# A three-layer graph network on one core: root products and last node blocks at other steps, lots in another spacing, and two matrices of each lot made on ScalarE

## The chip, the cores and the metric

The kernel runs on one core of a Trainium2 chip. The metric is the device time of one execution, in microseconds. The kernel before took 2903.43 us (median of three runs, 2900.62 to 2906.98). Engines are named as in the profile: PE is TensorE (PEld its weight loads), DVE VectorE, ACT ScalarE, POOL GpSimd, SP SyncE. On POOL this kernel does almost nothing but issue indirect DMAs, 128 rows each.

## What is computed

The graph has 6,250 nodes with 256 features and 100,000 edges, sorted by their destination. Each edge has a source, a destination, 32 attributes and one of three types. Three layers follow each other, and a layer norm ends it:

```python
ew = edge_attr @ edge_w + edge_b                      # 100000 x 256, the same in all layers
for l in range(3):
    residual = x
    msg = relu(x[src] * ew)
    out = 0
    for i in range(3):                                # the edge types
        h = segment_sum(msg * (edge_type == i), dst, n)
        out = out + (h * inv_cnt[i]) @ weights[l, i]
    x = residual + relu(out + x @ roots[l] + biases[l])
return layernorm(x_in + x)
```

The destinations are drawn as 6250 u², so that early nodes have many edges and late nodes few: a block of 128 nodes at the front takes dozens of edge pairs, one at the end takes three or four.

## The kernel before

**Pairs, quads and steps.** A tile is 128 edges, a pair two tiles, a quad two pairs. A layer is a loop over steps `it`; `reduce` at step `it` treats the pair `order[it]`. Everything that the pair needs is done a fixed number of steps earlier, in the same loop:

- `gather` (nine steps ahead): two indirect DMAs on POOL (line 1378) bring the source rows of `x` into the tile `xs`; eight quads of buffers (`ROWS`) are there.
- `seed_ew` (six ahead): ACT fills a PSUM tile `ew_p`, in layer 0 with the bias (L789), later with the kept `ew` that SP loaded from DRAM (L786).
- `make_ew` (five ahead, layer 0 only): PE adds the attribute product (L815); `keep_ew` (four ahead): ACT copies it out (L771, L765), and SP stores it.
- `weigh` (three ahead): DVE multiplies `xs` by `ew_p` (L838), ACT takes the relu (L839).
- `one_hot` (two ahead): DVE compares an iota with the destination and type of each edge, one 128x120 instruction for each tile (L852).
- `reduce`: PE multiplies messages and one-hot into the PSUM tile `h_p`, either with the one-hot as weights ("turned" spans, L870, then `take` on ACT, L886, and `turn` on PE, L890) or with the messages as weights (L878). A span is a run of pairs that share one place in `h_p`; `add` on DVE (L918) adds it to `acc`.

**The zone and the lots.** The 26 quads of the first 52 pairs hit very few nodes. In layer 0 their `ew` rows are scattered by POOL into a table in DRAM (L733), sorted by the source node's block and the type. Layers 1 and 2 read them back as 39 "lots" of up to four tiles: all edges of a tile have their source in one block of `x_all`, which is in SBUF. A lot so needs no gather. For a lot, PE spreads the source numbers over partitions (`seed_ew`, L781), `choose` on DVE compares them with the partition number (L794, tile `hot`, one 128x512 instruction), `expand` on PE picks the rows of `x_all` (L801), `weigh` and `one_hot` follow as for other quads (the one-hot reads a column of the tile `zone`). A lot takes two steps of the loop (some one), in which POOL has nothing to issue.

**Node blocks.** When all edges of a block of 128 nodes are added (`starts[c]` is the step), `node_mul` on PE (L947) multiplies the block's sums by the weights in two parts, at steps s and s+2; `node_end` on DVE (L978, L981) scales and adds them at s+2 and s+4, updates `x_all`, and SP writes the block to `x_mid` in DRAM (L984), the rows that the next layer gathers. Blocks are at least four steps apart. Block 48 is the short last one (106 rows), block 1 is finished after all others. The first six pairs of the next layer (twelve gathers, `gather_early`) wait for all blocks but 1, and a product on PE adds block 1's rows to them (`complete`, L830, L832); the gathers after these twelve wait for block 1's write too. In layer 2 there is a norm in place of the write (L987 to L1001).

**Root products.** `x @ roots` of a block is a transpose on PE (`root_turn`, L923) at its step, a copy on ACT two steps on (L927), a product on PE three on (`root_mul`, L931), and an addition on DVE six on (`root_keep`, L934). One PSUM buffer serves them all. Products are six steps apart at least; 22 results are held.

**What sets the order.** No scheduler moves instructions: each engine issues them as the loop writes them. The steps come from functions at the end of the file: `places_of` (between which pairs the zone's quads and the lots go), `spans_of`, `stages` (when a span is taken, turned and added), `schedule` (the order and `starts`). Layer 0 has 391 steps, layers 1 and 2 have 414 each.

## Time and profile before

| | |
|---|---|
| median of three runs | 2903.43 us |
| the profiled execution | 2903.96 us, span 2902.2 us, granted clock 0.948 |
| layer 0, by the gathers on POOL | from the start to 1142 us |
| layer 1 | 1159 to 2008 us |
| layer 2 | 2018 to 2883 us, then the last 19 us without a gather |
| indirect DMAs on POOL | 1332 + 770 + 24 + 12 gathers and 104 scatters, 2242 in all |

A row of a group reads: line, engine, operation, tile written <- tiles read, shape, count | busy time in us, mean ns of one | idle time of the engine before them, and what ended most of it. A row of the timeline reads: start, duration, engine, line, operation, tiles, and in brackets the idle time before it and what ended that. In a table of windows each row is a stretch of time, with the busy us and the number of instructions (x) of each engine.

### The profile page before, as it was taken

Reading aid. Unit: us, or ns where it says so; the run is one execution under the profiler, and the core shown is the slowest. Engines: PE = TensorE matmul, PEld = TensorE weight load, DVE = VectorE, ACT = ScalarE, POOL = GpSimd, SP = SyncE. Lnnn points to the kernel's source line nnn. Section 1 sums busy time; section 2 is a strip of 40 time slices with the busy share of each in tenths; the row PEclk is TensorE's granted clock in tenths of the full one; section 3 lists DMA queues with packets and bytes.
Section 4 is the critical chain, followed back from the end, with each engine's and each line's share of the span. In section 5 each row is a group of like instructions: output and inputs, shape, how many; then the busy total and the mean of one; then the engine's idle time right before and its main releaser. Section 6 shows DMA issues by size and latency. Waiting matters only on the chain. (4 is left out here: it accounts for less than half of the span.)

```text
span 2902.2 us, 44132 instructions
## 1 busy us (share of the span) xinstructions
PE 2409.1 (83%) x13302; PEld 1880.6 (65%) x13302; DVE 2207.5 (76%) x5612; ACT 1708.1 (59%) x2220; POOL 2138.6 (74%) x2253
## 2 busy tenths in 40 slices
PE   5799988888988789788898888777888888878776
PEld 2466656555666566577777777665666767767665
DVE  7777766766656576677878888776788888888986
ACT  5677766666666667455655555444555555555654
POOL 7676777777777775777777777776777777767775
PEclk9899998999889999999999999898999999999998
DMA  7898665556555666887777777676777777777765
GB/s 237 280 328 272 207 198 190 189 185 196 185 192 187 196 211 202 267 262 240 256 242 243 246 237 257 215 223 195 269 255 262 255 256 240 244 227 233 249 227 156
DMA packets 285411, 668.25 MB, mean 230 GB/s; under 512 B 50555, under 2 KB 142509, under 8 KB 285165
## 3 DMA queue, kind: packets, MB, share of 16 engines
q1 hardware_dynamic: 170112, 362.98, 35.9%
q0 software_dynamic: 107616, 294.11, 33.9%
q10 hardware_dynamic: 7436, 8.24, 0.9%
q8 instruction: 110, 1.80, 0.3%
q14 instruction: 137, 1.11, 0.1%
HBM read 528.50 MB, written 136.63 MB: 229 GB/s over the span
## 5 line engine op out<-in xcount | busy, mean ns | idle before, releaser
L1378 POOL DMA_INDIRECT xs<-x_mid,src_r x1332 | 1265.3, 950 | 420.1 <-issue 343.1
L1378 POOL DMA_INDIRECT xs<-in_x_dram,src_io x770 | 734.9, 954 | 243.1 <-issue 211.8
L839 ACT ACTIVATE xs<-xs 128x1024 f32<-128x1024 f32 x533 | 559.5, 1050 | 582.8 <-DVE xs L838 561.0
L838 DVE TENSOR_TENSOR xs<-ew_p,xs 128x1024 f32<-128x1024 f32 x533 | 646.5, 1213 | 314.3 <-ACT keep L771 176.3
L878 PE MATMUL h_p<-oh,xs 128*128 128x120 f32 x4768 | 692.5, 293 | 202.7 <-DVE acc L918 105.4
L878 PEld LDWEIGHTS h_p<-oh,xs 128*128 128x128 f32 x4768 | 641.3, 203 | 304.9 <-DVE acc L918 112.4
L852 DVE TENSOR_SCALAR oh<-iota_w,seg_o 128x120 f32<-128x120 f32 x2138 | 568.2, 328 | 0.0
L870 PE MATMUL h_p<-xs,oh 128*120 128x256 f32 x1868 | 517.7, 405 | 41.5 <-issue 14.7
L947 PE MATMUL o_p<-w_sb,acc 128*128 128x256 f32 (+1 forms) x1752 | 456.1, 397 | 64.8 <-DVE x_root L978 56.6
L918 DVE TENSOR_TENSOR acc<-h_p,acc 128x240 f32 (+1 forms) x764 | 338.9, 445 | 113.5 <-PE o_p L947 45.7
L947 PEld LDWEIGHTS o_p<-w_sb,acc 128*128 128x128 f32 (+1 forms) x1752 | 323.6, 195 | 141.5 <-DVE x_root L978 73.9
L870 PEld LDWEIGHTS h_p<-xs,oh 128*120 128x120 f32 x1868 | 319.5, 189 | 146.6 <-issue 30.0
L786 ACT ACTIVATE ew_p<-ew_s 128x1024 f32<-128x1024 f32 (+1 forms) x340 | 343.3, 1010 | 12.7 <-DMA ew_s<-ew_all 12.7
L771 ACT ACTIVATE keep<-ew_p 128x1024 f32<-128x1024 f32 x170 | 173.2, 1019 | 226.1 <-issue 115.5
L978 DVE SCALAR_TENSOR_TENSOR x_root<-o_p,inv,x_root 128x256 f32<-128x256 f32 (+1 forms) x438 | 210.5, 480 | 43.0 <-PE o_p L947 36.1
L839 ACT ACTIVATE zone<-zone 128x1024 f32<-128x1024 f32 (+1 forms) x78 | 78.8, 1010 | 223.9 <-DVE zone L838 223.9
L815 PE MATMUL ew_p<-ew_sb,at 64*128 64x512 f32 x630 | 199.0, 710 | 11.8 <-ACT ew_p L789 11.7
L789 ACT ACTIVATE ew_p<-seed 128x1024 f32<-128x1024 f32 (+1 forms) x194 | 198.5, 1023 | 0.0
L931 PE MATMUL r_p<-r_sb,t_s 128*128 128x256 f32 x588 | 158.7, 392 | 21.7 <-ACT t_s L927 21.4
L838 DVE TENSOR_TENSOR zone<-ew_p,zone 128x1024 f32<-128x1024 f32 (+1 forms) x78 | 90.6, 1162 | 107.5 <-PE ew_p L801 107.3
L870 PE MATMUL h_p<-zone,oh 128*120 128x256 f32 x576 | 148.0, 387 | 11.6 <-DVE acc L918 7.0
L801 PE MATMUL ew_p<-x_all,hot 128*128 128x256 f32 x588 | 150.6, 401 | 7.6 <-DVE hot L794 7.4
(178 smaller groups left out, 2340.8 us busy)
## 6 DMA issues: line engine op xcount, KB each, us to landing
ew_s<-ew_all SPq DMA_DIRECT2D x338, 512.0 KB
ew_all<-keep SPq DMA_DIRECT2D x169, 512.0 KB
zone<-zone_table SPq DMA_DIRECT2D x72, 516.0 KB
xs<-x_mid,src_r POOLq DMA_INDIRECT x1332
zone_table<-blank SPq DMA_DIRECT2D x21, 677.2 KB
xs<-in_x_dram,src_io POOLq DMA_INDIRECT x770
x_mid<-x_all SPq DMA_DIRECT2D x96, 128.0 KB
at<-in_attr_laid_dram SPq DMA_DIRECT2D x40, 256.0 KB
```

The costliest lines, as they stand in the source:

```text
L786: nc.scalar.activation(ew_ps[q][:, :n], ew_ss[q][:, :n], AF.Copy)
L789: nc.scalar.activation(ew_ps[q][:, :n], seed[:, None, None, :].to_broadcast([P, n, 2, D]), AF.Copy)
L815: nc.tensor.matmul(ew_ps[q][:, k].rearrange("p i d -> p (i d)"), at[half, :], ew_sb[half].rearrange("p i d -> p (i d)"), start=False, stop ...
L838: nc.vector.tensor_mul(there, ew_ps[q][:, pairs.start:pairs.stop, :n], there)
L839: nc.scalar.activation(there, there, AF.Relu)
L852: nc.vector.tensor_scalar(ohs[q][:, i, :], iota_w[:, :, :WIN], at, None, op0=ALU.is_equal)
L870: nc.tensor.matmul(h_p[:WK, :D], ohs[u // 2][:, t, :], rows_of(u, i), start=(i == 0 and first), stop=(i == n - 1 and closes(u)), skip_grou ...
L878: nc.tensor.matmul(h_p[:, d * WK:(d + 1) * WK], rows_of(u, i)[:, d * P:(d + 1) * P] if d < DC else full_ones, (ohs if d < DC else oh_bs)[u ...
L918: nc.vector.tensor_tensor(there, h_ps[span][:, :CH * WK].rearrange("p (c r w) -> p c r w", c=CH, r=R), there, op=ALU.add)
L947: nc.tensor.matmul(o_p[:n, j, :], acc[:, d, r, slot:slot + n], w_sb[:, r * DC + d, :], start=(d == 0), stop=(d == DC - 1))
L978: nc.vector.scalar_tensor_tensor(root, o_p[:n, j, :], inv[:n, c, r:r + 1], root, op0=ALU.mult, op1=ALU.add)
L1378: nc.gpsimd.indirect_dma_start(out=xs[:, u % 2, i, :], out_offset=None, in_=x_rows[:, :], in_offset=bass.IndirectOffsetOnAxis(ap=src_i[:, ...
```

## The change

**Root products of layer 0.** They stood at steps 5, 11, 17 and on, six apart, the last at 293. Now they stand at 20, 27, 34 and on, seven apart, the last at 356. In layers 1 and 2 the rule is the old one.

**Last blocks.** The blocks 44 to 48 are done at a quicker pace: `paces` gives 1 for them and 2 for the others; the second part follows after one step instead of two, the end after two instead of four, and the blocks are three steps apart. In layer 0 block 48 starts at step 378 (382 before) and ends at 380 (386 before). In layers 1 and 2 it starts at 402 (405) and ends at 404 (409), while block 0 moves from step 319 to 352. A new border at pair 60 cuts the last span, which ran over seven pairs (58 to 65): now (58, 60) stands alone and (60, 66) is a turned span. In layers 1 and 2 both are added one step after the point where the one was, and block 1 starts at 416 instead of 415. The span of the pairs' upper end (390, 391) is added at once.

**Lots.** Up to the 20th the places are nearly the old ones. From there the distance grows faster: before, the 30th lot stood before pair 254 and the 39th before pair 310; now they stand before 260 and 342. Before pair 288 or at it there were 36 lots, now 34.

**Matrices of a lot.** `choose` and, for lots, `one_hot` leave DVE. ACT computes relu(1 - |a - b|), which is 1 where two whole numbers are equal and 0 elsewhere: for `choose` one Abs and one Relu over 128x512, for the one-hot an Abs of 128x120 for each tile and one Relu over all (128x480).

```diff
@@ choose
-            nc.vector.tensor_scalar(hot[q][:, :n].rearrange("p i e -> p (i e)"),
-                                    ew_ps[q][:, 0].rearrange("p i d -> p (i d)")[:, :n * P],
-                                    node_i[:, 0:1], None, op0=ALU.is_equal)
+            there = hot[q][:, :n].rearrange("p i e -> p (i e)")
+            nc.scalar.activation(there, ew_ps[q][:, 0].rearrange("p i d -> p (i d)")[:, :n * P], AF.Abs, bias=node_i[:, 0:1], scale=-1.0)
+            nc.scalar.activation(there, there, AF.Relu, bias=one_f, scale=-1.0)
@@ one_hot
+            if q in zone:
+                for i in range(n):
+                    nc.scalar.activation(ohs[q][:, i, :].rearrange("p (r w) -> p r w", r=R), iota_w[:, :, :WIN], AF.Abs,
+                                         bias=zone[q][:, i // 2, i % 2, D:D + 1], scale=-1.0)
+                nc.scalar.activation(ohs[q][:, :n], ohs[q][:, :n], AF.Relu, bias=one_f, scale=-1.0)
+                return
@@ layer
+        next_at = {s + paces(c, NT): c for s, c in node_at.items()}
+        over_at = {s + 2 * paces(c, NT): c for s, c in node_at.items()}
...
-            step = max(3 + int((steps - 110) * (1 - (1 - j / NT) ** 0.5)), max(root_at, default=-1) + 6)
+            step = ROOT_AT + ROOT_EVERY * j if l == 0 else 3 + int((steps - 110) * (1 - (1 - j / NT) ** 0.5))
+            step = max(step, max(root_at, default=-1) + 6)
...
-            if it - 2 in node_at:
-                node_end(node_at[it - 2], 0)
-            if it - 4 in node_at:
-                node_end(node_at[it - 4], 1)
...
+            if it in next_at:
+                node_end(next_at[it], 0)
+            if it in over_at:
+                node_end(over_at[it], 1)
...
-LOT_SPACE = 4.5
-LOT_MORE = 0.04
+LOT_RATE = 0.215
+LOT_SLOWER = 0.000264
+ROOT_AT = 20
+ROOT_EVERY = 7
+QUICK = 5
@@ spans_of
-    stops = {K, last, middle, *quads, *lots}
+    stops = {K, last, last + 2, middle, *quads, *lots}
@@ stages
+        if spans[group[-1]][1] == -(-E // 256):
+            by = 0
@@
+def paces(c, NT):
+    return 1 if c >= NT - QUICK else 2
@@ schedule
-        step = starts[c] = max(done[c] + 2, step + 4)
+        step = starts[c] = max(done[c] + paces(c, NT), step + 2 + paces(max(c - 1, 2), NT))
```

Line numbers of the changed kernel are a few higher: L870 is L878 there, L878 is L886, L923 is L931, L978 is L986, L838 is L840, L786 is L788, L839 is L841.

**Where instructions move: PE, early in layer 0** (`h_s` is the copied span, `x_all` the nodes' features, `oh` the one-hot). Before:

```order
L815 MATMUL ew_p<-ew_sb,at 128x512 x2
L890 MATMUL h_p<-ident_o,h_s 128x120 x2
L892 MATMUL h_p<-ident_o,h_s 128x120
L923 MATMUL r_p<-ident_o,x_all 128x128 x2
L870 MATMUL h_p<-xs,oh 120x256
```

The same place now:

```order
L817 MATMUL ew_p<-ew_sb,at 128x512 x2
L898 MATMUL h_p<-ident_o,h_s 128x120 x2
L900 MATMUL h_p<-ident_o,h_s 128x120
L878 MATMUL h_p<-xs,oh 120x256
L881 LDWEIGHTS oh_b
```

The first root product's transposes are gone from step 5; they stand at step 20 now.

**DVE, at the end of layer 1** (the rows with 106x256 are block 48, the last `x_all` with 128x256 is block 1). Before:

```order
L978 SCALAR_TENSOR_TENSOR x_root<-o_p,inv,x_root 106x256 x2
L981 SCALAR_TENSOR_TENSOR x_all<-x_root,x_all 106x256
L852 TENSOR_SCALAR oh<-iota_w,seg_o 128x120 x4
L844 TENSOR_TENSOR xs<-ew_p,xs 128x256 x2
L910 TENSOR_LOAD place_i
L918 ISA
L918 TENSOR_TENSOR acc<-h_p,acc 128x6x40
L978 SCALAR_TENSOR_TENSOR x_root<-o_p,inv,x_root 128x256
```

Now block 48's end is followed by whole quads:

```order
L986 SCALAR_TENSOR_TENSOR x_root<-o_p,inv,x_root 106x256
L918 TENSOR_LOAD place_i
L926 ISA
L926 TENSOR_TENSOR acc<-h_p,acc 128x6x40
L986 SCALAR_TENSOR_TENSOR x_root<-o_p,inv,x_root 106x256 x2
L989 SCALAR_TENSOR_TENSOR x_all<-x_root,x_all 106x256
L860 TENSOR_SCALAR oh<-iota_w,seg_o 128x120 x4
L840 TENSOR_TENSOR xs<-ew_p,xs 128x1024
```

And this is the end of the layer now:

```order
L846 TENSOR_TENSOR xs<-ew_p,xs 128x256 x2
L918 TENSOR_LOAD place_i
L926 ISA
L926 TENSOR_TENSOR acc<-h_p,acc 128x6x40
L926 ISA
L926 TENSOR_TENSOR acc<-h_p,acc 128x6x40
L986 SCALAR_TENSOR_TENSOR x_root<-o_p,inv,x_root 128x256
```

Block 48's end stood just ahead of the last pair's product; two whole quads and a half come after it now, and there are two last additions instead of one.

**ACT, around a lot in the first part of layer 2.** Before:

```order
L886 ACTIVATE h_s<-h_p 120x256 x2
L839 ACTIVATE zone<-zone 128x4x256
L786 ACTIVATE ew_p<-ew_s 128x1024
L839 ACTIVATE xs<-xs 128x1024
L786 ACTIVATE ew_p<-ew_s 128x1024
```

The lot of the same number now:

```order
L841 ACTIVATE xs<-xs 128x1024
L797 ACTIVATE hot<-ew_p,node_i 128x512
L798 ACTIVATE hot<-hot,one_f 128x512
L788 ACTIVATE ew_p<-ew_s 128x1024
L841 ACTIVATE zone<-zone 128x4x256
L788 ACTIVATE ew_p<-ew_s 128x1024
L854 ACTIVATE oh<-iota_w,zone 128x120 x4
L856 ACTIVATE oh<-oh,one_f 128x480
L841 ACTIVATE xs<-xs 128x1024
```

`choose` stands behind the relu of the quad before the lot, the one-hot behind the lot's own relu and a seed, and the next quad's relu behind that.

More of the change, by code (lines that the diff above doesn't have):

```diff
@@ L691, in layer @@
         steps = len(order)
-        soon = min(SOON, steps - max(starts[:1] + starts[2:]) - 5)
+        soon = min(SOON, steps - starts[0] - 5, *(steps - starts[c] - 2 * paces(c, NT) - 1 for c in range(2, NT)))
         taken, turns, added, banks = stages(N, E, share, l)
@@ L1035, in layer @@
                 step = max(used[c], max(given_at, default=0) + 2)
-                assert step <= starts[c] + 2, (c, step, starts[c])
+                assert step <= starts[c], (c, step, starts[c])
                 given_at[step] = c
@@ L1227, in places_of @@
     quads = [K + ZONE_AT + int(ZONE_SPACE * j) for j in range(zone_of(N, E) // 2)]
-    lots = [K + LOT_AT + int(LOT_SPACE * j + LOT_MORE * j * j) for j in range(len(lots_of(N)))]
+    lots = [K + LOT_AT + int((LOT_RATE - (LOT_RATE ** 2 - 4 * LOT_SLOWER * j) ** 0.5) / (2 * LOT_SLOWER))
+            for j in range(len(lots_of(N)))]
     return [w + w % 2 for w in quads], [w + w % 2 for w in lots], K + MIDDLE_AT
```

20 lines of the change are left out of this document (11 added, 9 removed).

## The prediction, made before the change was run

> **What bounds the kernel now.** The page comes first.
>
> ```profile
> PE 2409.1 (83%) x13302; PEld 1880.6 (65%) x13302; DVE 2207.5 (76%) x5612; ACT 1708.1 (59%) x2220; POOL 2138.6 (74%) x2253
> ...
> L1378 POOL DMA_INDIRECT xs<-x_mid,src_r x1332 | 1265.3, 950 | 420.1 <-issue 343.1 <-DMA xs<-x_mid,src_r 15.2 <-ACT xs L839 12.6
> L1378 POOL DMA_INDIRECT xs<-in_x_dram,src_io x770 | 734.9, 954 | 243.1 <-issue 211.8 <-DMA xs<-in_x_dram,src_io 6.1 <-PE ew_p L815 5.2
> ```
>
> PE looks the busiest, but POOL's gathers are the bound: each takes 0.95 us, and 0.30 us of issue stand before the next, so one starts every 1.25 us. 2242 indirect DMAs at 1.25 us are 2803 us of a span of 2902. The other 99 us are what can be won: some 4 ahead of the first gather, some 19 behind the last, and about 75 in which POOL waits for the rest. POOL's timeline shows where. First layer 0:
>
> ```profile
> 105.04 0.94 POOL L1378 DMA_INDIRECT xs<-in_x_dram,src_io  x1 [7.43 <-issue]
> ...
> 293.82 1.00 POOL L733 DMA_INDIRECT zone_table<-keep,slot_i  x1 [11.48 <-ACT keep L765]
> ```
>
> then the borders of the layers:
>
> ```profile
> 1141.30 0.95 POOL L1378 DMA_INDIRECT xs<-in_x_dram,src_io  x1 [0.30 <-issue]
> 1159.06 0.94 POOL L1378 DMA_INDIRECT xs<-x_mid,src_e  x1 [16.81 <-DMA x_mid<-x_all]
> ...
> 1174.06 0.94 POOL L1378 DMA_INDIRECT xs<-x_mid,src_r  x1 [0.30 <-issue]
> ```
>
> ```profile
> 2007.43 0.95 POOL L1378 DMA_INDIRECT xs<-x_mid,src_r  x1 [0.30 <-issue]
> 2017.61 0.95 POOL L1378 DMA_INDIRECT xs<-x_mid,src_e  x1 [9.23 <-issue]
> ...
> 2032.60 0.95 POOL L1378 DMA_INDIRECT xs<-x_mid,src_r  x1 [0.30 <-ACT ew_p L786]
> ```
>
> Beyond the 0.30 these are 7.1 and 11.2 us in layer 0, 16.5 and 8.9 at the borders. The windows show the rest:
>
> ```profile
> core 0: us, PE busy (x) PEld busy (x) DVE busy (x) ACT busy (x) POOL busy (x), PEclk, DMA share, GB/s
> 105.00:294.00 189.00, 173.84 (x907) 114.81 (x904) 148.33 (x395) 144.91 (x196) 133.76 (x142) 0.99 0.88 291
> ...
> 2190.00:2400.00 210.00, 180.43 (x916) 146.60 (x915) 174.57 (x437) 122.79 (x184) 159.11 (x168) 0.98 0.78 253
> 2400.00:2620.00 220.00, 179.72 (x1145) 158.60 (x1145) 190.66 (x492) 118.64 (x157) 155.81 (x165) 0.98 0.74 242
> ```
>
> From 2190 to 2400 POOL issues 168 in 210 us, one in 1.25: nothing lost. From 2400 to 2620 it issues 165 where 176 would fit: 11 x 1.25 = 14 us lost. Why there, and not before, the distance from a quad's last gather to its product tells (counted off in the timeline, a gather and the product that belongs to it):
>
> ```profile
> 2187.44 0.95 POOL L1378 DMA_INDIRECT xs<-x_mid,src_r  x1 [0.30 <-issue]
> ...
> 2574.00 0.95 POOL L1378 DMA_INDIRECT xs<-x_mid,src_r  x1 [0.30 <-issue]
> ```
>
> ```profile
> 2197.75 1.22 DVE L838 TENSOR_TENSOR xs<-ew_p,xs 128x1024 f32<-128x1024 f32 x1
> ...
> 2608.91 1.22 DVE L838 TENSOR_TENSOR xs<-ew_p,xs 128x1024 f32<-128x1024 f32 x1
> ```
>
> At step 90 of layer 2 the product comes 10.3 us after the gather, at step 290 34.9 us: compute falls behind by 25 us and by the 14 that POOL stood still, because the eight buffers were full. The 200 steps took 411 us, 2.06 a step. A lot takes two steps in which POOL needs no time. In layer 1, whose DVE has no norm, the same place stays below the limit, 17.6 us:
>
> ```profile
> 1719.02 0.95 POOL L1378 DMA_INDIRECT xs<-x_mid,src_r  x1 [0.30 <-issue]
> ```
>
> ```profile
> 1736.60 1.22 DVE L838 TENSOR_TENSOR xs<-ew_p,xs 128x1024 f32<-128x1024 f32 x1
> ```
>
> **The change part by part.** The gathers and scatters stay as many, so only waits can change.
>
> *Root products of layer 0.* Up to 294 us PE is 92% busy and sets the pace; the scatter at 293.82 waits until compute reaches step 96. Up to there 16 root products stood, now 11.
>
> ```profile
> L931 PE MATMUL r_p<-r_sb,t_s 128*128 128x256 f32 x588 | 158.7, 392 | 21.7 <-ACT t_s L927 21.4
> ...
> L923 PE MATMUL r_p<-ident_o,x_all 128*128 128x128 f32 x294 | 64.5, 302 | 66.6 <-DVE x_root L934 65.4 <-DMA xs<-in_x_dram,src_io 0.8
> ```
>
> One costs PE (158.7 + 64.5) / 147 = 1.5 us: five fewer are 7.6. At six steps the next transpose also waits for DVE's addition of the one before (65.4 us in the run, most of it in layers 1 and 2, where the spacing stays); at seven it doesn't. Both waits of POOL are compute's backlog and together 18 us. I take -8, between -2 (DVE, with its sort, sets the pace) and -15. Nine products now stand behind step 293, where PE has slack until 1060; POOL's lead covers them. If that cover is gone, they cost at the border.
>
> *First border.* Block 48 is done six steps earlier, 6 x 2.5 = 15 us by POOL's pace, so its write lands about when the last gather is issued, and the 16.5 us of waiting go. Late next is block 1:
>
> ```profile
> 1154.36 10.56 SPq L984 DMA_DIRECT2D x_mid<-x_all  x2
> ```
>
> The first of these two writes is block 48's; the gather that waits for it starts at 1159.06, 4.7 us later. Block 1's is issued at 1164.6 and so lands at about 1169.3. The thirteenth gather needs it; it started at 1174.06. So 4.8 us can be won, less the turn of the new span on PE (a few transposes):
>
> ```profile
> L890 PE MATMUL h_p<-ident_o,h_s 120*128 120x120 f32 x514 | 88.0, 275 | 1.4 <-ACT h_s L886 1.4
> ```
>
> and an addition, about 1 us. I take -4; 0 if PE falls behind at the end of layer 0 because of the root products, -8 if block 1 profits from block 48's being out of the way.
>
> *Second border.* Without the wait, the twelve gathers begin at 2008.7 and end at 2023.7.
>
> ```profile
> 2005.08 16.09 SPq L984 DMA_DIRECT2D x_mid<-x_all  x3
> ```
>
> ```profile
> 2020.39 0.42 DVE L981 SCALAR_TENSOR_TENSOR x_all<-x_root,x_all 128x256 f32<-128x256 f32 x1
> ```
>
> Block 1's write goes out at 2020.8 and lands at about 2025.5. That is 7 us before 2032.60; DVE no longer has block 48's end ahead of the last product (about 2.4 us), but two additions. I take -8, from -5 to -9.
>
> *The tail.* The same exchange stands at the end of layer 2: 0, from -1.5 to +1.5.
>
> *Lots: spacing.* Two or three lots fewer stand before step 290 of layer 2, each 2 x 2.06 = 4.1 us of compute: about 10 of the 14 us. Later ones stand ten to twelve steps apart, where POOL's time for eight to ten pairs (20 to 25 us) and compute's (10 to 12 steps at 2.06) are about equal, so nothing is given back.
>
> *Lots: the matrices on ACT.* What DVE loses, and the nearest rows for ACT:
>
> ```profile
> L771 ACT ACTIVATE keep<-ew_p 128x1024 f32<-128x1024 f32 x169 | 172.6, 1021 | 226.1 <-issue 115.5 <-DMA zone_table<-keep,slot_i 77.7 <-PE ew_p L815 11.8
> ...
> L852 DVE TENSOR_SCALAR oh<-iota_w,zone 128x120 f32<-128x120 f32 x294 | 78.5, 328 | 0.0
> ...
> L927 ACT ACTIVATE t_s<-r_p 128x256 f32<-128x256 f32 x147 | 53.9, 367 | 0.0
> ...
> L794 DVE TENSOR_SCALAR hot<-ew_p,node_i 128x512 f32<-128x512 f32 x72 | 53.5, 743 | 2.2 <-PE ew_p L781 2.2
> ...
> L993 ACT ACTIVATE mv<-mv,eps 128x1 f32<-128x1 f32 x48 | 13.5, 281 | 1.5 <-DVE mv L989 1.5
> ```
>
> From 256 to 1024 elements an ACTIVATE grows by 0.85 ns each; one with a bias from a tile and one element takes 281. An Abs or Relu of 120 so takes 383 ns, of 480 690, of 512 717, and a lot of four tiles 4 x 383 + 690 + 2 x 717 = 3.7 us on ACT, for the 1.8 us that leave DVE. In the window 2190:2400, with 14 lots, ACT goes from 122.8 to 174 us of 210 (83%), DVE from 174.6 to 149 (71%), PE stays at 86%. The total fits. The Trainium skill's page "ScalarE: Activation LUTs" (Rules for kernel authors) speaks against it: such work belongs on VectorE. By its "What ACT_TABLE_LOAD costs" (280 ns + 0.833 ns an element with a bias operand) a lot would cost an estimated 3.6 us; the rows agree, and the sum would be the same.
>
> What matters is the queue. A lot in the timeline:
>
> ```profile
> 2297.69 0.74 DVE L794 TENSOR_SCALAR hot<-ew_p,node_i 128x512 f32<-128x512 f32 x1
> 2297.81 1.06 ACT L839 ACTIVATE xs<-xs 128x1024 f32<-128x1024 f32 x1 [3.43 <-DMA xs<-x_mid,src_r]
> ...
> 2300.71 1.89 PE L801 MATMUL ew_p<-x_all,hot 128*128 128x256 f32 x8
> ...
> 2307.11 1.89 PE L870 MATMUL h_p<-zone,oh 128*120 128x256 f32 x8
> ```
>
> The choosing matrix was ready at 2298.4; now it follows the relu (to 2298.9) and takes 1.4, so 2300.3, just ahead of PE at 2300.7. The one-hot now follows expand (to 2302.6), product 1.2, relu 1.1, seed 1.0 and its own 2.2: 2308.1, where PE reduced from 2307.1: PE would wait 1 us, and the takes and relus queued behind it on ACT are late by as much. Against that DVE is 1.8 us sooner at each lot. I take +0.2 us a lot over the 24 lots between steps 90 and 290, about 5 us of backlog, from -1 to +1 a lot. So of layer 2's 14 us, 10 by spacing, less 5 by ACT, rounded with the few us lost at 2521 to 2580: -8, from -15 to +14.
>
> **Sum:** -8 -4 -8 +0 -8 = -28, 2903.96 - 28 = 2876 us for an execution like the profiled one, which is within 0.5 us of the median.
>
> **The rivals.**
> *All waits go* (0.2): the relief of DVE outweighs ACT's queue and the 14 us go whole, the terms at their better ends: -15 -8 -9 -1.5 -15, about 2858 with some of it overlapping. For it speaks DVE's 87% in 2400:2620.
> *The borders keep their cost* (0.15): PE, which now does root products late in layer 0, brings block 1 later, and early in layer 0 DVE's sort sets the pace: -2 +0 -5 +0 -5, 2892. Against it speaks PE's slack before 1060.
> *ACT holds up PE at every lot* (0.1): with 2 us a lot instead of 0.2 the backlog before step 290 grows by 24 x 2 = 48 in both layers. Layer 2 then loses 48 - 10 = 38 us more; layer 1 reaches 17.6 - 10 + 48 = 56, 21 above the 34.9 that the buffers hold. -20 + 38 + 21 = +39: 2943. It beats the gains from 30 / 24 = 1.25 us a lot on.
> *Gains and ACT's queue cancel* (0.05): 1.25 us a lot, 2904.
>
> **How the numbers follow.** 0.5 for the forecast, with 2866 to 2888 as its own range. About 0.2% (6 us) is what a measurement of this kernel can tell from no change. Faster by more: the forecast, the first two rivals, 0.85; same 0.05; slower 0.1. The range, 2856 to 2898, holds the first three cases and leaves out most of the last two.
>
> **What would show it.** Right: POOL's wait at the first border under 2 us with a new one, 2 to 8 us, ahead of the thirteenth gather; scatter's wait at 294 us halved; 170 or more gathers in layer 2's last third of lots where 165 stood; ACT near 80% in the lots. Wrong: PE idle before the reduce of a lot for over a microsecond each time, ended by ACT's one-hot, and POOL's waits spread over layers 1 and 2; or block 48's write still the last to end the first border's wait.

## The result and the profile after

The changed kernel takes 2945.86 us (median of four runs, 2942.89 to 2955.99), the kernel before beside it 2905.2 us (four runs, 2900.62 to 2908.48): a ratio of 1.0147, 95% interval 1.0117 to 1.0177 (the two medians alone give 1.0140). It is slower by 1.5% where 1% less was forecast. The profiled execution took 2943.04 us, with a span of 2941.1, 39 us more than the one of before.

POOL's timeline of the changed kernel has the same places as before's: the scatter at the start of layer 0, the two borders with the first gather and the thirteenth, and the last gather.

```profile
292.52 1.00 POOL L735 DMA_INDIRECT zone_table<-keep,slot_i  x1 [11.48 <-ACT keep L767]
...
1142.94 0.98 POOL L1400 DMA_INDIRECT xs<-in_x_dram,src_io  x1 [0.30 <-issue]
1156.40 0.95 POOL L1400 DMA_INDIRECT xs<-x_mid,src_e  x1 [12.48 <-ACT ew_p L791]
...
1174.25 0.94 POOL L1400 DMA_INDIRECT xs<-x_mid,src_r  x1 [3.13 <-PE r_p L832]
...
2017.05 0.95 POOL L1400 DMA_INDIRECT xs<-x_mid,src_r  x1 [0.30 <-issue]
2018.30 0.96 POOL L1400 DMA_INDIRECT xs<-x_mid,src_e  x1 [0.31 <-ACT xs L841]
...
2033.36 0.95 POOL L1400 DMA_INDIRECT xs<-x_mid,src_r  x1 [0.31 <-issue]
...
2911.25 0.95 POOL L1400 DMA_INDIRECT xs<-x_mid,src_r  x1 [0.30 <-issue]
```

Set against before, the scatter is 1.3 us earlier (293.82), the thirteenth gather of layer 1 starts 0.2 us later (1174.06), that of layer 2 0.8 later (2032.60), the last gather 29.2 later (2882.1), and from the last gather to the end of the span it takes 29.9 us instead of 20.1. Step by step: layer 0 with the first border +0.2, layer 1 +9.5, the second border -8.9, layer 2's gathers +28.4 and the tail +9.8, together the 39 us.

The windows of the prediction, after:

```profile
core 0: us, PE busy (x) PEld busy (x) DVE busy (x) ACT busy (x) POOL busy (x), PEclk, DMA share, GB/s
105.00:294.00 189.00, 172.24 (x898) 113.45 (x896) 146.70 (x390) 143.00 (x195) 132.85 (x141) 0.98 0.89 292
2190.00:2400.00 210.00, 178.29 (x878) 141.38 (x877) 147.09 (x351) 159.74 (x272) 153.54 (x162) 0.98 0.76 248
2400.00:2620.00 220.00, 176.17 (x1056) 154.93 (x1055) 166.90 (x421) 141.18 (x217) 148.17 (x156) 0.94 0.69 224
```

From 2400 to 2620 POOL issues 156 gathers where 165 stood; 170 or more were forecast. DVE has 167 us of work there instead of 191. PE is nearly as busy as before (176 us, before 180), but gets through 1056 matmuls instead of 1145; a part of its time runs at a lower clock (0.94, before 0.98).

The groups of instructions around a lot, first of the kernel before, then of the changed one (behind the bar: busy time, mean ns, then idle time and what ended it):

```profile
L870 PE MATMUL h_p<-zone,oh 128*120 128x256 f32 x576 | 148.0, 387 | 11.6 <-DVE acc L918 7.0 <-ACT xs L839 2.3 <-ACT ew_p L786 1.6
...
L801 PE MATMUL ew_p<-x_all,hot 128*128 128x256 f32 x588 | 150.6, 401 | 7.6 <-DVE hot L794 7.4
...
L839 ACT ACTIVATE zone<-zone 128x1024 f32<-128x1024 f32 (+1 forms) x78 | 78.8, 1010 | 223.9 <-DVE zone L838 223.9
```

```profile
L878 PE MATMUL h_p<-zone,oh 128*120 128x256 f32 x576 | 156.8, 402 | 55.6 <-ACT oh L856 49.2 <-DVE acc L926 6.1
L803 PE MATMUL ew_p<-x_all,hot 128*128 128x256 f32 x588 | 149.3, 397 | 30.6 <-ACT hot L798 30.3
...
L841 ACT ACTIVATE zone<-zone 128x1024 f32<-128x1024 f32 (+1 forms) x78 | 78.7, 1009 | 191.6 <-DVE zone L840 191.6
```

PE waits 56 us for the lots' one-hot where it waited 12, and 31 for the choosing matrices where it waited 8. The last row of each says why: ACT stands idle ahead of the lot's relu, because DVE's product isn't there, 192 us now (2.5 us a lot) and 224 us before. Before, PE needed nothing else of this lot that stood behind that idle time; now the one-hot does. It needs neither the product nor the relu, it only stands behind them. One lot in ACT's and PE's timelines:

```profile
2287.99 1.06 ACT L841 ACTIVATE zone<-zone 128x1024 f32<-128x1024 f32 x1 [0.91 <-DVE zone L840]
2288.96 1.01 ACT L788 ACTIVATE ew_p<-ew_s 128x1024 f32<-128x1024 f32 x1
2289.91 1.23 ACT L854 ACTIVATE oh<-iota_w,zone 128x120 f32<-128x120 f32 x4
2291.17 0.69 ACT L856 ACTIVATE oh<-oh,one_f 128x480 f32<-128x480 f32 x1
...
2291.92 1.99 PE L878 MATMUL h_p<-zone,oh 128*120 128x256 f32 x8 [1.14 <-ACT oh L856]
```

### The profile page after: what moved, and what is told of

Its sections match the earlier page's. It is cut to its first block, busy times and chain, and to the rows that moved or that the text cites. A ratio compares the mean times of both kernels' runs of the same rounds, so it can differ in the third digit from the quotient of the medians.

```text
span 2941.1 us, 44007 instructions
## 1 busy us (share of the span) xinstructions
PE 2422.7 (82%) x13250; PEld 1885.8 (64%) x13250; DVE 2094.3 (71%) x5245; ACT 1931.5 (66%) x2751; POOL 2144.5 (73%) x2253
## 5 line engine op out<-in xcount | busy, mean ns | idle before, releaser
L886 PE MATMUL h_p<-oh,xs 128*128 128x120 f32 x4648 | 681.1, 293 | 197.7 <-DVE acc L926 93.1
L841 ACT ACTIVATE xs<-xs 128x1024 f32<-128x1024 f32 x533 | 558.0, 1048 | 420.4 <-DVE xs L840 405.7
L840 DVE TENSOR_TENSOR xs<-ew_p,xs 128x1024 f32<-128x1024 f32 x533 | 645.7, 1211 | 254.6 <-ACT keep L773 173.5
L886 PEld LDWEIGHTS h_p<-oh,xs 128*128 128x128 f32 x4648 | 632.2, 203 | 289.2 <-issue 113.8
L878 PE MATMUL h_p<-xs,oh 128*120 128x256 f32 x1928 | 530.2, 404 | 52.6 <-DVE acc L926 17.2
L878 PEld LDWEIGHTS h_p<-xs,oh 128*120 128x120 f32 x1928 | 328.0, 188 | 167.3 <-issue 38.9
L788 ACT ACTIVATE ew_p<-ew_s 128x1024 f32<-128x1024 f32 (+1 forms) x340 | 343.4, 1010 | 10.5 <-DMA ew_s<-ew_all 10.5
L986 DVE SCALAR_TENSOR_TENSOR x_root<-o_p,inv,x_root 128x256 f32<-128x256 f32 (+1 forms) x438 | 210.5, 481 | 86.7 <-PE o_p L955 79.1
L840 DVE TENSOR_TENSOR zone<-ew_p,zone 128x1024 f32<-128x1024 f32 (+1 forms) x78 | 90.7, 1162 | 183.1 <-issue 103.7
L817 PE MATMUL ew_p<-ew_sb,at 64*128 64x512 f32 x630 | 197.7, 705 | 16.4 <-ACT ew_p L791 15.8
L841 ACT ACTIVATE zone<-zone 128x1024 f32<-128x1024 f32 (+1 forms) x78 | 78.7, 1009 | 191.6 <-DVE zone L840 191.6
L878 PE MATMUL h_p<-zone,oh 128*120 128x256 f32 x576 | 156.8, 402 | 55.6 <-ACT oh L856 49.2
L791 ACT ACTIVATE ew_p<-seed 128x1024 f32<-128x1024 f32 (+1 forms) x194 | 198.5, 1023 | 0.0
L939 PE MATMUL r_p<-r_sb,t_s 128*128 128x256 f32 x588 | 166.6, 407 | 16.4 <-ACT t_s L935 15.2
L803 PE MATMUL ew_p<-x_all,hot 128*128 128x256 f32 x588 | 149.3, 397 | 30.6 <-ACT hot L798 30.3
```

The lines of the kernel that those rows point to most:

```text
L788: nc.scalar.activation(ew_ps[q][:, :n], ew_ss[q][:, :n], AF.Copy)
L791: nc.scalar.activation(ew_ps[q][:, :n], seed[:, None, None, :].to_broadcast([P, n, 2, D]), AF.Copy)
L817: nc.tensor.matmul(ew_ps[q][:, k].rearrange("p i d -> p (i d)"), at[half, :], ew_sb[half].rearrange("p i d -> p (i d)"), start=False, stop ...
L840: nc.vector.tensor_mul(there, ew_ps[q][:, pairs.start:pairs.stop, :n], there)
L841: nc.scalar.activation(there, there, AF.Relu)
L878: nc.tensor.matmul(h_p[:WK, :D], ohs[u // 2][:, t, :], rows_of(u, i), start=(i == 0 and first), stop=(i == n - 1 and closes(u)), skip_grou ...
```

## The experiments

Each ratio is to the kernel before, run beside it on the same chip, with its 95% interval. "Layer 2's loss" is what POOL's gathers of layer 2 wait beyond the 1.25 us spacing, counted where one is over 0.1 us late (17.9 us before, 44.5 in the changed kernel; the 28.4 above is the plain difference of the two stretches). The tail is the time from the start of the last gather to the end.

**Order or matrices.** Three theories are named in the expectations: Order (the new steps are what costs), Load (ACT is simply fuller, wherever its new work stands) and Queue (what costs is that the matrices stand late in ACT's queue, behind work that itself waits).

*The order alone.* Both matrices of a lot back on DVE:

```diff
 def choose(q):
-    nc.scalar.activation(there, ..., AF.Abs, bias=node_i[:, 0:1], scale=-1.0)
-    nc.scalar.activation(there, there, AF.Relu, bias=one_f, scale=-1.0)
+    nc.vector.tensor_scalar(hot..., ew_ps..., node_i[:, 0:1], None, op0=ALU.is_equal)
 def one_hot(q):
-    if q in zone: ...  # both activations
```

> The changed kernel with both matrices of the lots back on VectorE: root products, last blocks and lots in the new order, nothing else. Queue theory (the matrices stand late in ScalarE's queue and PE waits for them; the order by itself gains the second border's wait and part of layer 2's): 2885 to 2895 us, and PE's waits of 49 us for the one-hot and 30 us for the choosing matrix are gone. Order theory (the rival: the quick last blocks and the lots' spacing cost, ScalarE's work is free): 2935 to 2950 us.

Measured: 2926.33 us, 1.0087 (1.0071 to 1.0104). The order by itself loses 24 us, which lies between the two theories' ranges: neither the order nor the matrices are free. The second border's wait is gone, as forecast, but layer 2 loses 33.6 us and the tail takes 30.6.

*The matrices alone.* The order of before, both matrices on ACT as in the change.

> The kernel before with only the two matrices of the lots moved to ScalarE, all in the old order. Queue theory: 2945 to 2965 us, since the lots stand denser before step 290 of layer 2 than in the new order, and the first border's and second border's waits stay. Order theory: 2895 to 2905 us.

Measured: 2939.5 us, 1.0128 (1.0106 to 1.0150). The matrices alone lose 37 us, a little less than the Queue theory had, and layer 2's loss takes 26 of them (44.2 against 17.9). The two parts don't add (24 and 37 alone, 41 together): layer 2 loses 33.6 us with the one, 44.2 with the other and 44.5 with both.

*The choosing matrix alone on ACT.* The new order, the one-hot back on DVE.

> The changed kernel with the one-hot of the lots back on VectorE; only the choosing matrix stays on ScalarE. Queue theory: PE's 49 us of waits for the one-hot go, the 30 us for the choosing matrix stay or shrink: 2895 to 2920 us. Order theory: 2935 to 2950 us. Load theory (ScalarE's total time counts, not the place in its queue): of 3.7 us a lot 1.4 stay, so 0.4 of the loss: 2905 to 2915 us.

Measured: 2935.37 us, 1.0104 (1.0087 to 1.0121), 9 us over the order alone. This is above the ranges of Queue and Load and in that of Order, since the order has lost 24 us already; the late one-hot adds some 10 more here.

*The one-hot one step sooner.* The whole change, with ACT's one-hot ahead of the lot's relu in ACT's queue:

```diff
+            if pair(3) is not None and first_of(it + 3, 2) and pair(3) >= ZU:
+                one_hot(pair(3) // 2)
             if pair(3) is not None and first_of(it + 3, 2):
...
-            if pair(2) is not None and first_of(it + 2, 2) and pair(2) // 2 != order[-1] // 2:
+            if pair(2) is not None and first_of(it + 2, 2) and pair(2) // 2 != order[-1] // 2 and pair(2) < ZU:
```

> The changed kernel with the same work on ScalarE, but the one-hot of a lot issued one step sooner, ahead of the lot's own relu, where ScalarE otherwise waits for VectorE's product (192 us in all for the lots). Queue theory: PE's wait for the one-hot falls from 49 us to under 10, the time to 2895 to 2920 us. Load theory and order theory: no change, 2935 to 2950 us.

Measured: 2912.15 us, 1.0034 (1.0020 to 1.0049). Moving this one call takes back 31 of the 41 us (33 by the ratios), with ACT's work unchanged. A lot in this kernel, and its groups:

```profile
2267.54 1.25 ACT L854 ACTIVATE oh<-iota_w,zone 128x120 f32<-128x120 f32 x4
2268.82 0.69 ACT L856 ACTIVATE oh<-oh,one_f 128x480 f32<-128x480 f32 x1
2269.43 1.04 ACT L841 ACTIVATE zone<-zone 128x1024 f32<-128x1024 f32 x1
...
2271.24 1.96 PE L878 MATMUL h_p<-zone,oh 128*120 128x256 f32 x8
```

```profile
L803 PE MATMUL ew_p<-x_all,hot 128*128 128x256 f32 x588 | 158.8, 416 | 34.5 <-ACT hot L798 34.3
L878 PE MATMUL h_p<-zone,oh 128*120 128x256 f32 x576 | 148.2, 386 | 6.0 <-DVE acc L926 5.4 <-ACT xs L841 0.7
...
L841 ACT ACTIVATE zone<-zone 128x1024 f32<-128x1024 f32 (+1 forms) x78 | 78.6, 1008 | 63.1 <-DVE zone L840 62.6
```

The one-hot now fills the wait for DVE's product (ACT's idle time ahead of the relu falls from 192 to 63 us), and PE's wait for it is gone (6.0 us are left, for other things). For the one-hot the Load theory falls. The choosing matrix still holds PE (34.3 us): it stands behind the relu of the quad before the lot, and a sooner place for it wasn't tried.

**Which part of the order, and ACT in the former order.** Two more theories: Lots (the lots' new places are what the order loses by) and Blocks (it is the last blocks' closer steps).

*The lots at their former places*, in the new order, matrices on DVE:

```diff
-    lots = [K + LOT_AT + int((LOT_RATE - (LOT_RATE ** 2 - 4 * LOT_SLOWER * j) ** 0.5) / (2 * LOT_SLOWER)) ...]
+    lots = [K + LOT_AT + int(LOT_SPACE * j + LOT_MORE * j * j) ...]
```

> The new order with both lot matrices on VectorE (2926.3 us in this series, ratio to the kernel before 1.0087), and in it the lots alone at their former places (last lot of layers 1 and 2 at step 314 instead of 346). Lots theory: the new spacing leaves some six lots for the last 100 steps of layer 2, beside the ends of the blocks and the norm, and that is where the new order loses; with the old places layer 2's gathers lose 18 us again instead of 34, and the tail from the last gather to the end falls from 30.6 to about 21 us, so 2897 to 2905 us, ratio 0.998 to 1.001. Blocks theory: it is the last five blocks' closer steps (and the earlier turn of the last span) that cost; then this kernel stays at 2920 to 2928 us with a tail near 30 us, or goes higher by the stall that the spacing was to remove.

Measured: 2900.82 us, 0.9982 (0.9971 to 0.9993). All that the order lost was in the lots' places; without them the new order gains 0.2%, though the tail takes 25.0 us and not the 21 that the Lots theory had. Its second border, in POOL's timeline (the last gather of layer 1 and the first early one):

```profile
2003.39 0.95 POOL L1393 DMA_INDIRECT xs<-x_mid,src_r  x1 [0.30 <-issue]
2004.64 0.95 POOL L1393 DMA_INDIRECT xs<-x_mid,src_e  x1 [0.30 <-issue]
```

*The blocks at their former pace* (`QUICK = 0`), in the new order, matrices on DVE.

> The new order with both lot matrices on VectorE, and in it the last five blocks at the former pace (two steps between a block's stages, four between blocks), the rest of the order as changed. Blocks theory: the tail goes back from 30.6 to about 21 us and the time to 2912 to 2917 us, less if layer 2's wait goes too, and the second border loses some of its 10 us. Lots theory: 2924 to 2930 us, with the tail still near 30 us and layer 2's gathers still losing over 30 us, since the late lots are still there.

Measured: 2928.09 us, 1.0078 (1.0060 to 1.0096): the same as the order alone. The second border's wait is back (10.4 us), layer 2's loss is 32.7, and the tail is 25.2 instead of 30.6. Closer blocks gain at the border and lose half of that in the tail.

*The former order, both matrices on ACT, the one-hot one step sooner.*

> The former order, with both lot matrices on ScalarE as in the change, but the lot's one-hot issued one step sooner, ahead of the lot's relu (in the new order this took 34 us away, 2945.9 to 2912.2 us). Queue theory: ScalarE's work is harmless once its results are in time, and VectorE's relief gains as it did in the new order against both on VectorE (2926.3 to 2912.2, -14 us); so 2885 to 2895 us, ratio 0.994 to 0.998, with layer 2's gathers losing under 18 us. Load theory: ScalarE's 3.7 us a lot delay takes, relus and write-outs wherever they stand, and the gain in the new order came only from lots that stood late; then 2903 to 2925 us.

Measured: 2910.49 us (2897.28 to 2919.43), 1.0016 (1.0002 to 1.0030). The Queue theory's gain didn't come, and the time lies in the Load theory's range. But the place in the queue counts here as in the new order: with the one-hot late, the same order had a ratio of 1.0128, some 33 us more.

*The same with the choosing matrix on DVE.*

> The former order with the lot's one-hot alone on ScalarE, one step sooner, and the choosing matrix on VectorE as before. In the new order the choosing matrix on ScalarE cost 9 us by itself (2935.4 against 2926.3). Queue theory: that cost falls away beside the run with both on ScalarE, so 2 to 9 us below it, 2880 to 2890 us. Load theory: half of ScalarE's extra load, so half of that run's loss, 2903 to 2914 us.

Measured: 2900.11 us, 0.9978 (0.9968 to 0.9988), 10 us below the run before, as much as the choosing matrix cost in the new order (9). So of the two matrices the one-hot is worth moving, if it stands early; the choosing matrix isn't, in the place that it had. The gain is 6 us, though, not the 12 to 22 that the Queue theory had, and the time lies between the two theories' ranges: VectorE's relief is worth less than thought.

**Adding up, and the places of the lots.**

*Both gains.* The new order with the former lots, ACT making the one-hot early, DVE the choosing matrix.

> What has gained so far, together: the new order with the lots at their former places (2900.8 us, 0.998), and in it the lot's one-hot alone on ScalarE one step sooner (which by itself, in the former order, gave 2900.1 us, 0.998). If the two act at different places (the second border's 10 us; layer 2's stall, which the one-hot brought from 18 to 7 us), the gains add: 2885 to 2893 us, ratio 0.992 to 0.996. If both only change when the one compute backlog of layer 2 meets the eight buffers, they do not add: 2896 to 2902 us.

Measured: 2888.99 us, 0.9948 (0.9934 to 0.9962). They add. This kernel beats both, the one before by 13 us and the changed one by some 57.

*As that, the closer blocks in layers 0 and 1 only* (`return 1 if c >= NT - QUICK and l < 2 else 2`).

> As the kernel with both gains, but the last five blocks at the closer pace in layers 0 and 1 only, since layer 2 has no border behind it and its blocks there carry the norm. Blocks theory for the tail: the time from the last gather to the end goes back from 25 towards 21 us, so 3 to 5 us less than with the closer pace everywhere (2881 to 2889 us if the gains add). Rival: the tail is set by the two more additions behind the last reduction and by the turn of the split last span, which stay; then the same time within 2 us.

Measured: 2888.41 us, 0.9944 (0.9929 to 0.9958). The tail falls from 25.8 to 23.7 us, the time by no more than its scatter: the rival's "same within 2 us". The rest of the tail (before 20.1) would be the split last span and its additions, which nothing here tried alone.

*The new lots alone*, all else as before.

> The former kernel with the lots' new places alone (last lot of layers 1 and 2 at step 346 instead of 314, block 0 at step 352 instead of 319). Lots theory: the whole loss of the new order is in it, 20 to 28 us, so 2925 to 2935 us, ratio 1.007 to 1.010, with layer 2's gathers losing over 30 us, TensorE's clock in 2440 to 2800 us at half for 50 us or more instead of 24, and layers 0 and 1 as before. Rival: the places cost only together with the closer blocks or the split span; then 2900 to 2912 us. The prediction's own step would have it at 2893 to 2898 us.

Measured: 2920.77 us, 1.0064 (1.0048 to 1.0080): 18 us lost, a little less than the Lots theory had, and far from the prediction's gain.

*Denser lots*, `LOT_MORE = 0.02` in the kernel before.

> The opposite dose: the former kernel with the lots closer together (LOT_MORE 0.02 instead of 0.04: last lot at step 286, block 0 at 291). By the prediction's spacing step this is worse: two to three more lots before step 230 put the backlog against the eight buffers sooner, 8 to 12 us more stall in layer 2, 2912 to 2920 us. Lots theory (what stands late costs): the same time or less, 2890 to 2906 us, with the stall moved ahead and the clock after 2600 us higher.

Measured: 2931.92 us, 1.0092 (1.0075 to 1.0110). Denser is worse too, so "what stands late costs" falls as a rule. That is the direction of the prediction's spacing step, but 29 us where it had 8 to 12.

**Density or exact steps.** The Spacing theory has it that the number of lots in each part of the layer decides, the Meeting theory that the exact steps do, at which a lot meets the end of a block or other work. Three runs shift a list of places by two steps and keep its spacing; a fourth takes a spacing between the former and the new one. All are the kernel before with other places.

*The former list two steps later:*

```diff
-LOT_AT = 6
+LOT_AT = 8
```

> The former kernel with every lot two steps later, its spacing kept. Spacing theory (how many lots stand before and after the middle decides): a shift by one pair changes almost nothing, 2896 to 2908 us. Meeting theory (the exact steps at which a lot meets a block's end, a root product or an addition decide, and the former places happened to be good): 2915 us or more, with TensorE's clock in layer 2 at half for longer than the former kernel's 59 us.

Measured: 2916.29 us, 1.0048 (1.0031 to 1.0065).

*The former list two steps sooner*, from the seventh lot on (`- 2 * (j > 5)`).

> The former kernel with every lot from the seventh on two steps sooner, its spacing kept. Spacing theory: 2896 to 2908 us. Meeting theory: 2915 us or more, as with the shift the other way, or at least one of the two.

Measured: 2917.26 us, 1.0047 (1.0031 to 1.0064).

*The new list two steps later* (the new formula with `LOT_AT = 8`).

> The former kernel with the lots at the changed places (2920.8 us, 1.0064), all two steps later. Spacing theory: the same within 6 us, 2915 to 2927 us. Meeting theory: anywhere between 2895 and 2935 us; 2908 us or less would show that it was not the spacing that cost.

Measured: 2904.69 us, 1.0007 (0.9995 to 1.0018).

*A spacing between* (`LOT_MORE = 0.05`).

> The former kernel with LOT_MORE 0.05 (last lot at step 330, between 314 of before and 346 of the change). 0.02 gave 1.009, the change's places 1.006. Spacing theory, with an optimum between the two: a smooth curve, so 2898 to 2912 us. Meeting theory: no curve, and by chance 2910 to 2930 us.

Measured: 2907.67 us, 1.0017 (1.0007 to 1.0027). This one lies in the Spacing theory's range and below the Meeting theory's; the three shifts came as the Meeting theory had them.

The former list loses 14 us when shifted either way, the new one wins 16 when shifted by two steps. The spacing is the same on both sides of each comparison, so it isn't the spacing that costs there: the exact steps do, and the former places are good ones. In the main the ratios go with the time that compute takes for steps 204 to 336 of layer 2 (between DVE's products, interpolated to the step), most of it a stretch in which the eight buffers are full and POOL waits; the denser list loses more than its row says, since it reaches step 204 some 12 us late already.

```text
kernel                          steps 204-336, us   layer 2's loss   ratio
former lots                           282.8              17.9        1
new lots, two later                   286.9              11.3        1.0007
between                               290.9              17.7        1.0017
former lots, two sooner               293.0              33.0        1.0047
denser                                293.8              41.8        1.0092
former lots, two later                295.8              26.4        1.0048
new lots                              303.1              31.6        1.0064
new order, new lots                   305.6              33.6        1.0087
new order, former lots                282.3              19.7        0.9982
```

One lot fewer stands between these steps in the new list (12 against 13), and compute takes 20 us longer there.

**Which meeting.** Counted over ten profiles with the matrices on DVE, the six steps around a lot in this stretch take 15.9 us on average where a block starts two steps behind the lot (18 lots), 13.5 where it starts with it (29) and 12.4 where it started two steps ahead (19), each with a spread of 1.3 to 2 us; with no block so near it is 13.2 (56). The new list has three lots of the first kind before step 336, the former none. The count doesn't order the whole table, though: the former list two steps sooner has five of them there and takes 293 us, two steps later it has one and takes 296. These three moved by two steps, in the kernel before with the new list, and in the whole change with the one-hot sooner:

```diff
     lots = [K + LOT_AT + int((LOT_RATE - (LOT_RATE ** 2 - 4 * LOT_SLOWER * j) ** 0.5) / (2 * LOT_SLOWER))
+            + 2 * (j in (26, 28, 36))
             for j in range(len(lots_of(N)))]
```

> The former kernel with the changed lots' places (2920.8 us, 1.0064), and of them the three before step 336 that stand two steps ahead of a block's start (212, 230 and 320, ahead of 214, 232 and 322) moved two steps later, on to that start; every block stays where it was. Counted over ten profiles, the six steps around a lot take 15.9 us where a block starts two steps behind it, and 13.5 us where it starts with it. Meeting theory: three lots in the stretch in which POOL waits for compute, each 2.5 to 3.5 us, and the half-clock windows that follow such waits; so 6 to 12 us less, 2907 to 2914 us, ratio 1.001 to 1.004. Rival: what costs is elsewhere in the new places; then 2918 us or more.

Measured: 3970.58 us beside 3967.4 of the kernel before, 1.0021 (0.9992 to 1.0050).

> The whole change, with the two faults that the runs point to mended: ScalarE's one-hot of a lot one step sooner (2912.2 us, 1.0034), and the same three lots moved two steps later. If the two add, 2900 to 2906 us, ratio 0.999 to 1.001, with layer 2's gathers losing 15 to 20 us instead of 26. Rival: with VectorE relieved the meeting no longer costs; then 2909 us or more.

Measured: 3942.25 us beside the same 3967.4, 0.9934 (0.9907 to 0.9960). These two ran on another chip, on which the kernel before itself took a third longer; in their own profiles the clock is 0.83 and POOL waits hundreds of microseconds in every layer. So neither can tell what sets the time in this stretch on the other chips. Which meeting costs stays open; the count is only a hint, and one lot of the shifted list that starts with its block (step 214 there) took 16.4 us as well.

## TensorE's clock, an amplifier

Look at one stretch of time in layer 2: PE's busy time is about the same in all these kernels, and the work that it does in it isn't. The windows from 2440 to 2800 us, of before, of the order alone, and of the order with the former lots:

```profile
2440.00:2640.00 200.00, 160.65 (x1016) 141.46 (x1015) 173.17 (x451) 107.64 (x143) 140.86 (x148) 0.97 0.73 239
2640.00:2800.00 160.00, 127.99 (x797) 111.50 (x798) 144.74 (x392) 95.23 (x125) 121.12 (x128) 0.96 0.74 237
```

```profile
2440.00:2640.00 200.00, 160.79 (x934) 142.09 (x934) 161.59 (x419) 102.12 (x135) 131.22 (x139) 0.90 0.68 220
2640.00:2800.00 160.00, 124.37 (x751) 108.98 (x751) 137.05 (x371) 87.69 (x117) 119.13 (x126) 0.93 0.71 228
```

```profile
2440.00:2640.00 200.00, 163.59 (x1023) 144.46 (x1022) 176.31 (x464) 110.43 (x149) 140.16 (x148) 0.96 0.72 236
2640.00:2800.00 160.00, 125.08 (x769) 108.86 (x768) 140.88 (x382) 93.27 (x123) 121.01 (x129) 0.95 0.74 235
```

160 us of PE are 1016 matmuls before and 934 with the new order. The clock's records have two values, 1 and 0.5, and the half clock comes in multiples of 3.41 us. It adds up to 24 us before between 2440 and 2800, 65 with the order alone, 34 with its former lots, 58 with the matrices alone, 55 in the changed kernel, 44 with the one-hot sooner. It doesn't order all kernels: the quickest of all (closer blocks in layers 0 and 1 only) has 41 us there. In finer windows of the order alone it shows what sets it off:

```profile
core 0: us, PE busy (x), PEclk, DMA share, GB/s
2613.69:2617.10 3.41, 3.41 (x22) 1.00 1.04 328
2617.10:2620.50 3.40, 3.40 (x29) 1.00 0.98 381
2620.50:2623.92 3.42, 1.12 (x10) 1.00 0.36 107
2623.92:2630.75 6.83, 6.07 (x20) 0.50 0.63 178
2630.75:2634.16 3.41, 2.81 (x20) 1.00 0.28 93
```

PE stood idle 2.3 of 3.42 us, and in the next 6.8 us it got through 20 matmuls, as many as in the 3.4 us behind them at full clock. So one wait of PE of about 2 us costs up to another 1.7 us for each window at half clock behind it (an estimate, half of 3.41), where PE has work queued.

Windows of time hold different steps in different kernels. These hold steps 204 to 336 of layer 2, of before, of the matrices alone and of the order alone:

```profile
2425.20:2708.00 282.80, 228.17 (x1448) 0.98 0.74 238
```

```profile
2441.60:2738.70 297.10, 244.19 (x1450) 0.93 0.70 226
```

```profile
2419.30:2724.90 305.60, 239.56 (x1426) 0.92 0.69 222
```

With the matrices alone the lots are the same, and so is PE's work. PE was idle for 52.9 us, no more than before (54.6), but busy for 16 us more, and it ran at half clock for 44 us instead of 14: in these steps the whole loss is slower work. With the order alone there is one lot fewer. Even so PE was busy for 11 us more, at half clock for 51 us, and idle for 11 us more. That the waits come first is read from the windows; no run kept PE warm in the waits, so how much of the loss would be left without the half clock isn't shown. Counted over these steps, it is 14 us with the former lots, 24 to 34 with the shifted, the denser and the in-between lists and 41 with the new one, nearly the order of the table.

## Why the prediction was wrong

Two terms carry the miss: the lots' places, put at -10 (alone +18), and the matrices on ACT, put at +5 in layer 2 and at nothing elsewhere (alone +37). The tail, put at 0, adds 10.

- **What bounds the kernel** held: POOL's spacing stayed at 1.25 us in every profile but for waits, and the time went where POOL waited, in layer 2 above all.
- **Layer 0's root products, -8:** measured 1.3 us at the scatter in this profile. The mean of the scatter's start over the eight profiles with the new root products is 292.0 us (288.5 to 296.6), over ten with the former ones 294.1 (292.0 to 298.3), so that the gain is hardly clear of the scatter from profile to profile. PE had less to do up to there (172.2 us instead of 173.8) and the scatter's wait stayed at 11.48 us. The step had -2 as its less likely end, DVE setting the pace. That is the size that came; that DVE is the reason isn't shown.
- **First border, -4:** the wait fell by 4.3 us (16.8 to 12.5) and a new one of 2.8 came ahead of the thirteenth gather, just as the text had it, but the sum is -1.4, since block 1's write came 7 us later (1164.6 before). SP's queue after, block 48's write and block 1's:

```profile
1150.45 0.31 SPq L992 DMA_DIRECT2D x_mid<-x_all  x1
...
1171.69 0.32 SPq L992 DMA_DIRECT2D x_mid<-x_all  x1
```

  Block 48's went out 3.9 us sooner and no longer ends the wait; the row of the first early gather names ACT's seed of a quad of layer 0 (L791), so it is compute's backlog. Over the same eight and ten profiles the stretch from layer 0's last gather to the thirteenth takes 32.8 us with the new root products and 31.4 with the former. The step that failed is that block 1's write stays at 1164.6. The nine later root products, for which the text had "PE has slack until 1060; POOL's lead covers them", fit as the cause; no run moved them alone.
- **Second border, -8:** right. 8.9 us of waiting gone in the changed kernel, and back when the pace was undone.
- **The tail, 0:** measured +10. The closer blocks and the split last span put more compute behind the last gather (25.0 us with the former lots), and with the late lots it is 30.6. The late lots alone make only 21.8.
- **Lots' spacing, -10:** wrong in sign. "About equal, so nothing is given back" compared totals. With the new lots alone step 290 comes 15 us later after the layer's first gather (607.4 us, before 592.5), where the text had about 10 sooner. Compute's time for these steps isn't set by the number of lots alone; two steps' shift of the same list changes it by 16 us (303.1 and 286.9).
- **The matrices on ACT, +0.2 us a lot:** the queue was read rightly and the sum mis-sized. PE's wait was foreseen at 1 us for the one-hot and at none for the choosing matrix, and is 0.63 and 0.39 (49.2 and 30.3 over 78 lots). By the text's own measure, steps 90 to 290 of layer 2, the matrices alone cost 13.5 us (424.7 us instead of 411.2), 0.56 for each of the 24 lots, which is within its range of -1 to +1. But the twelve lots ahead of step 90 were not in the sum, and compute reaches that step 12.6 us later already (194.0 us after the layer's first gather, before 181.4). Together that is about the 26 us by which layer 2's loss grew. The credit, "DVE is 1.8 us sooner at each lot", came to little: with the matrices alone DVE waits, between 2190 and 2750 us, 42 us for the norm's step on ACT and the blocks' products on PE, where it waited 19, and even with the one-hot put early its relief was worth 6 us. And PE's slower work behind its waits, 16 us in steps 204 to 336, was no term at all.
- **The rival of 2943 us**, ACT holding up PE at every lot (0.1), has the measured time, but not by its sum: PE waited 1 us and not 2, layer 1 lost 9.5 us and not 21, and the order alone loses 24 of the 41 us.
- ACT's time was nearly right: a lot takes 1.23 + 0.69 + 0.67 + 0.72 = 3.3 us in the timeline, 3.7 forecast. The Trainium skill's page "ScalarE: Activation LUTs" (Rules for kernel authors) advises VectorE, not ScalarE, for operations such as relu, add and mul. For the choosing matrix, where it stood, the runs agree (9 to 10 us lost), for the one-hot, put early, they don't (6 us gained).

## What to carry to other kernels

In a queue that runs in order, look at what stands just ahead of the moved work and what that waits for: for the same 1.9 us of ACT a lot, a place behind a relu that waits for another engine and one ahead of it are 33 us apart, and only the second gains (6 us) over VectorE's making it. A formula for an order written out in steps has to be tried shifted by a step or two before its density is judged; here a shift alone was worth 14 to 16 us. And in a stretch that is short of compute, look at PE's waits of 2 us and more and at the granted clock behind them: its busy share grows when its work gets slower.

## What the runs showed of the hardware

PE's clock was more easily lost than expected. Over 18 profiles, all but those of the last two experiments, cut into the 3.41 us windows in which the clock's records change, between 300 and 2860 us: of 8171 windows in which PE was idle for under 0.5 us, 57 were followed by one at half clock, of 340 with 1.6 to 1.8 us of idling 105, of 288 with 1.8 to 2.0 us 233, and all 831 with 2.0 us or more. The way back is harder: no window at full clock with under 1.2 us of idling (9849) was followed by half clock, but of 156 windows at half clock with 0.5 to 1.2 us of idling 142 were followed by another; after all 853 without any, the clock was full. The Trainium skill's page "TensorE: Matmul & The Clock Gate" (What's actually happening) has the half clock come after at least one idle window of about 3.4 us; the two values and the length of the window agree with the records here, but a window idle for somewhat over half is enough.
